# A depthwise branch's 1x1 convolution moved into the preceding scan, and two of its nine taps moved to TensorE

## The chip, the cores and the metric

The kernel runs on one core of a Trainium2 chip. Five engines work side by side, each through its own instruction queue in order: TensorE (PE in the profile; PEld is its loading of weights), VectorE (DVE), ScalarE (ACT), GpSimd (POOL) and SyncE (SP), which here issues nearly all DMAs. The metric is the device time of one execution in microseconds. Before the change it is 19043.21 us, the median of 3 runs (19038.22 to 19052.77).

## The reference

The input is x, eight images of 384 channels and 64 x 64 pixels, in float32. Two layers follow each other, both with a residual.

```python
# layer 0: channel attention on a group-normalised input
q = dwconv3x3(conv1x1(gn(x), wq), dwq)      # the same for k and v
attn = softmax(l2norm(q) @ l2norm(k).T * temperature)   # 8 heads, 48 x 48
x = x + conv1x1(attn @ v, wproj)

# layer 1: selective scan in four directions k
xs = cross_scan(gn(x))                      # rows, columns, and both reversed
dt, B, C = split(x_proj[k] @ xs)            # 12 + 16 + 16 rows
h = h * exp(dt * A) + dt * u * B            # along 4096 positions, 16 states a channel
y = sum over states of h * C, plus D * u, merged over the four directions
x = x + gelu(layernorm(y))
```

## The kernel before

For each image `channel_attention` and then `selective_scan` run. The order on each engine is written out by hand: every compute instruction is pinned to program order. x stays in SBUF as three tiles of 128 channels (NJ = 3).

**Attention.** The work is cut into 36 pieces of 16 image rows and 128 channels: 12 for k, 12 for q (each 128 channels, then four row groups), then 12 for v (each row group, then three channel groups). KQ is 24, the first v piece. The loop over t is a pipeline: in iteration t, `bands` and `band` make the 1x1 convolution of piece t+2 (three products of 512 columns on PE per eight rows, then an eviction with bias on ACT, L370 and L374) into the tile `pre`; `start_sum` and `end_sum` prepare piece t+1 (three or four whole-tile products by a tap's weight on ACT, L419, the center tap straight into the PSUM accumulator `ac`, and two additions on POOL); `finish_sum` ends piece t on DVE, with five taps as multiply-add (L457) and an addition (L462). For v, 18 rows of all three channel groups make one `pre`; two of its rows are copied from the one before. In the q and k pieces, transposes, Gram products and statistics of the previous image's output (`load_last`, tile `fs`) go along. In the v pieces the previous image's output is finished (`finishing`: loads `fy`, transposes, GELU, a POOL addition, the store), attention is projected (`project_in`, L603, and `project_out`, L610, a DVE addition), and the next image's statistics are taken from loads into qT and gm (`load_ahead`). The weights are scaled by the normalisation's 1/std (`scale_weights`), and `shift_of` makes the matching bias: nine products of one column on PE and one 128x3 instruction on DVE.

**Scan.** 32 steps (four directions of eight chunks of 512 positions), each of 12 units (three channel groups by four groups of four states). In unit u, POOL makes `db` for the next unit (L950), ACT the decays `da` (`decay`, L938), DVE four scans `h` (L962), PE the transposes of the previous unit's h (`turned`, L983), ACT copies them out (`kept`, L989, tile hc), and PE multiplies them by C (`added`, L1000; on two blocks of every fourth unit of directions 0 and 2, a `skip` product more). `weigh` makes w = x * dt (L921). Units 0 to 5 also hold the projection of the next step on PE (`project`), unit 6 its eviction (`lay_out`), and unit 9 is a burst: the next step's step sizes with two ACT table loads, the four `cp` tiles on DVE, and two of the three moves of y (`take`). One PSUM bank (`ps_m`, tag m) serves `px`, `pct` and the shift in turn. `look_ahead` prepares k's weights of the next image: the load in step 2, three scalings and the shift in step 3.

What sets the order around the change is this hand-written order and the buffers' release: nothing is scheduled later by a tool. SP's queue, too, issues in program order and waits there for what a DMA needs.

## Time and profile before

| What | Value |
|---|---|
| Median of 3 runs | 19043.21 us |
| Profiled execution, its own time | 19037.42 us |
| Its span, first to last instruction | 19035.6 us |
| Mean granted PE clock | 0.968 |
| Busy DVE, ACT, PE, POOL | 96%, 93%, 90%, 89% of the span |
| DMA | 1842.96 MB, mean 97 GB/s |
| One image: attention, then scan (image 1) | 417.1 us, 1951.7 us |

Busy time is the union of an engine's instructions. A busy share over the span is a mean over stages with different limits, so the stages are read one by one with a table of stretches: each row gives the stretch in microseconds from the span's start, its length, and busy time with the count of instructions for PE, PEld, DVE, ACT and POOL, then the granted clock of PE, the share of the 16 DMA engines in use and the rate. The view of waits gives, for an instruction, what ended the idle time before it: total, how often, the longest. The timeline gives start, length, engine, line, operation, tiles and count, and in brackets the idle time before it with what ended it. A float32 product shows as two matmul records, a transpose as one.

### The profile page before, as it was taken

The page shows a single profiled execution, that of the slowest core. Times are in us where ns is not written, and L with a number is a line of the kernel's source. Part 1 is how long each engine was busy: PE and PEld are TensorE (multiplying, and loading weights), DVE is VectorE, ACT ScalarE, POOL GpSimd, SP SyncE. Part 2 cuts the span into 40 slices and gives each one's busy share as a digit, 9 for nine tenths or more (in the row PEclk, how much of TensorE's full clock was granted, in tenths as well). Part 3 has the DMA queues.
Part 4 walks back from the last instruction along what each step waited for, and adds up shares of the span by engine and source line. Part 5 has one row for each costly group of instructions (what it writes and reads, how often), then busy time and mean ns, then how long its engine had stood idle before and what let it go on. Part 6 is the DMA issues. An engine that isn't in the chain of part 4 may idle for free. (4 is left out here: it accounts for less than half of the span.)

```text
span 19035.6 us, 415284 instructions
## 1 busy us (share of the span) xinstructions
PE 17213.2 (90%) x166560; PEld 9804.2 (52%) x166560; DVE 18353.2 (96%) x17552; ACT 17725.0 (93%) x29821; POOL 16891.1 (89%) x7491
## 2 busy tenths in 40 slices
PE   7999989999899998999989999899998999989998
PEld 4555545555455554555545555455554555545554
DVE  8999989999899998999989999899998999989999
ACT  6999979999799997999979999799997999979998
POOL 4999959999599995999959999599995999959998
PEclk9999999999999999999999999999999999999999
DMA  1233332333323333233332333223333233322333
GB/s 58 87 100 100 103 99 86 99 100 103 102 83 100 99 104 105 83 96 100 109 99 89 94 97 107 99 90 98 96 104 100 89 100 100 98 88 88 100 99 118
DMA packets 1199753, 1842.96 MB, mean 97 GB/s; under 512 B 154400, under 2 KB 1014816, under 8 KB 1060608
## 3 DMA queue, kind: packets, MB, share of 16 engines
q1 hardware_dynamic: 1196960, 1816.28, 29.8%
q8 instruction: 1314, 21.53, 0.5%
q14 instruction: 615, 5.04, 0.1%
q10 hardware_dynamic: 864, 0.12, 0.0%
HBM read 1497.29 MB, written 318.77 MB: 95 GB/s over the span
## 5 line engine op out<-in xcount | busy, mean ns | idle before, releaser
L950 POOL TENSOR_TENSOR db<-w,B 128x2048 f32<-128x2048 f32 x3072 | 14077.5, 4588 | 47.8 <-DVE h L962 24.9
L962 DVE TENSOR_TENSOR_SCAN h<-da,ca,db 128x512 f32<-128x512 f32 x10752 | 12723.9, 1265 | 30.7 <-ACT da L938 16.8
L983 PE MATMUL pt<-ident,h 128*128 128x128 f32 x49152 | 8164.9, 291 | 1079.4 <-ACT hc L989 882.1
L938 ACT ACTIVATE da<-dt,neg_a 128x512 f32<-128x512 f32 x12288 | 8616.7, 703 | 178.4 <-DVE h L962 171.3
L989 ACT COPY hc<-pt 128x512 f32<-128x512 f32 x12288 | 7265.4, 594 | 161.7 <-PE pt L983 77.0
L983 PEld LDWEIGHTS pt<-ident,h 128*128 128x128 f32 x49152 | 5324.2, 143 | 3958.9 <-ACT hc L989 2658.4
L1000 PE MATMUL py<-hc,cp 128*32 128x128 f32 x98304 | 5221.7, 289 | 1.2 <-ACT hc L989 1.2
L1000 PEld LDWEIGHTS py<-hc,cp 128*32 128x32 f32 x98304 | 1983.3, 109 | 2164.0 <-issue 2143.9
L962 DVE TENSOR_TENSOR_SCAN h<-da,db 128x512 f32<-128x512 f32 x1536 | 1739.5, 1209 | 65.1 <-ACT da L938 43.5
L426 POOL TENSOR_TENSOR pr<-pr,pr 128x1008 f32<-128x1008 f32 x288 | 673.1, 2337 | 1187.9 <-ACT pr L419 1156.8
L847 PE MATMUL px<-x,wx 128*44 128x128 f32 x6144 | 1580.2, 346 | 79.5 <-DVE cp L889 65.6
L921 POOL TENSOR_TENSOR w<-x,dt 128x512 f32<-128x512 f32 x744 | 1063.6, 1430 | 1.4 <-ACT dt L912 1.4
L847 PEld LDWEIGHTS px<-x,wx 128*44 128x44 f32 x6144 | 505.3, 120 | 663.5 <-issue 630.7
L904 PE MATMUL pd<-xd,wdt 128*128 128x512 f32 x1536 | 725.8, 608 | 97.5 <-DVE h L962 91.6
L432 POOL TENSOR_TENSOR pr<-pr,pr 128x1008 f32<-128x1008 f32 x288 | 574.9, 1996 | 230.7 <-ACT pr L419 165.2
L603 PE MATMUL pp<-v,mT 128*128 128x512 f32 x1152 | 545.7, 622 | 100.0 <-DVE v L462 98.9
L889 DVE TENSOR_TENSOR cp<-quad,pct 128x512 f32<-128x512 f32 x1024 | 630.4, 684 | 0.0
L976 POOL COPY ca<-h 128x4 f32<-128x4 f32 x2688 | 552.7, 206 | 0.0
L904 PEld LDWEIGHTS pd<-xd,wdt 128*128 128x128 f32 x1536 | 270.9, 189 | 397.4 <-issue 177.2
L912 ACT ACTIVATE dt<-pd,dt_bias 128x512 f32<-128x512 f32 x768 | 469.5, 679 | 2.1 <-PE pd L904 1.4
L1042 DVE TENSOR_TENSOR ys<-ys,py 128x512 f32<-128x512 f32 x576 | 388.5, 674 | 38.6 <-PE py L1000 38.6
L603 PEld LDWEIGHTS pp<-v,mT 128*128 128x128 f32 x1152 | 219.2, 198 | 359.3 <-issue 232.5
(337 smaller groups left out, 11426.5 us busy)
## 6 DMA issues: line engine op xcount, KB each, us to landing
B<-bcd SPq DMA_DIRECT2D x1024, 1024.0 KB, 5.1
yd<-ys SPq DMA_DIRECT2D x384, 256.0 KB, 5.3
ys<-yd SPq DMA_DIRECT2D x768, 128.0 KB, 3.0
yd<-ys SPq DMA_DIRECT2D x768, 128.0 KB, 5.2
x<-in_x SPq DMA_DIRECT2D x48, 1024.0 KB, 8.0
x1d<-x SPq DMA_DIRECT2D x192, 256.0 KB, 3.0
ys<-yd SPq DMA_DIRECT2D x192, 256.0 KB, 2.9
fy<-yd SPq DMA_DIRECT2D x128, 384.0 KB, 4.2
```

The lines of the kernel that those rows point to most:

```text
L426: pin(nc.gpsimd.tensor_add(q[:, :, 1:], q[:, :, 1:], left[:, :, : W - 1]))
L603: pin(nc.tensor.matmul(pps[m, c], lhsT=fold_of[0][:, j, bass.ts(m, P)], rhs=vs["v"][:, j, bass.ts(c, CH)], start=j == 0, stop=j == NJ - 1,))
L847: pin(nc.tensor.matmul(split(pxs[s][:XR, :])[:, part, :], lhsT=wx[:, j, k, :], rhs=view(x1[j], k, c)[:, part, :], start=i == 0, stop=i == ...
L889: pin(nc.vector.tensor_mul(t, m.broadcast_to([P, NQ, HP]), c.broadcast_to([P, NQ, HP])))
L904: pin(nc.tensor.matmul(pd, lhsT=wdt[:, k, bass.ts(j, P)], rhs=xds[s], start=True, stop=True))
L921: pin(eng.tensor_mul(split(ws[s, j]), view(x1[j], k, c), split(dts[s, j])))
L938: pin(nc.scalar.activation(t, dts[s, j], AF.Exp, scale=neg_a[:, j, steps[s][0], n : n + 1]))
L950: pin(eng.tensor_mul(t, w.broadcast_to([P, NV, CH]), bts[s, g]))
L962: pin(nc.vector.tensor_tensor_scan(h, da, db, 0.0 if start else carries[s - 1][:, j, n : n + 1], ALU.mult, ALU.add,))
L983: pin(nc.tensor.transpose(t[:, f, :], hs[u][:, bass.ts(q, HP), :].rearrange("p l v -> p (l v)"), ident))
L989: pin(nc.scalar.copy(t, pts.pop((u, lb))))
L1000: pin(nc.tensor.matmul(py[f * HP : (f + 1) * HP, lb, :], lhsT=cps[s, g][:, q, :], rhs=hc[:, f, :], start=g == lb == 0, stop=g == NG - 1 an ...
```

## The change

For all images but the first, v's 1x1 convolution is made during the scan of the image before. In steps 3 to 26 of that scan one product of 128 channels by 512 positions is made per step: an x chunk is loaded every third step in unit 2 (`v_load`), the three matmuls go at the ends of units 9, 10 and 11 (`v_product`), ACT evicts with the bias in unit 0 of the next step, and the result is stored to DRAM (`v_store`, tile v1d). Attention then loads windows of 18 rows from there (`load_v`) instead of computing bands. For these v pieces the center tap and the vertical neighbour go to PE as products with diagonal matrices (`add_by_pe`, tile `diag`, made by nine DVE instructions at the start of attention); ACT's center product and one of DVE's five taps are gone. wv is loaded, scaled and shifted in steps 0 to 3 of the scan, wk in steps 28 to 31, one scaling a step. Several buffers are fewer: hc 4 for 6, w 2 for 3, ysum 2 for 3 (its loads move to units 6, 7 and 10), the products' tag split into 2 and 2 for 4, the weights 1 for 2. In the scan's first step the third `weigh` moves from DVE to POOL.

```diff
@@ channel_attention
+            if v1_d:
+                diag = wp.tile([P, NJ, 3, P], F32, name=f"diag{b}")
+                for m in range(NJ):
+                    for k in range(3):
+                        pin(nc.vector.tensor_scalar_mul(
+                            diag[:, m, k, :], ident, dws["v"][:, m, 3 * k + 1 : 3 * k + 2]
+                        ))
+
             def load_w(n):
-                wts[n] = wp.tile([P, NJ, C], F32, tag="wt", bufs=2, name=f"{n}{b}")
+                wts[n] = wp.tile([P, NJ, C], F32, tag="wt", bufs=1 if v1_d else 2, name=f"{n}{b}")
...
+                if w == "v" and v1_d:
+                    return []
...
+            def load_v(p):
+
+                pres["v", p] = t = work.tile([P, L], F32, tag="pre", name=f"pre{b}v{p}")
+                r0, r1 = max(0, PR * p - 1), min(H, PR * (p + 1) + 1)
+                nc.sync.dma_start(
+                    t[:, : NJ * (PR + 2) * W].rearrange("p (m l) -> p m l", m=NJ)[:, :, : (r1 - r0) * W],
+                    v1_d[:, :, r0 * W : r1 * W].rearrange("m p l -> p m l"),
+                )
...
+            def add_by_pe(t):
+
+                pre, lo = rows_of(t)
+                m, y0 = pieces[t][1], PR * pieces[t][2] - lo
+                tap, dy, r0, r1 = far_tap(t)
+                for s, e in ((0, r0), (r0, BR), (BR, r1), (r1, PR)):
+                    both = r0 <= s and e <= r1
+                    for d, k in ((0, 4), (dy, tap))[: 1 + both] if e > s else ():
+                        pin(nc.tensor.matmul(
+                            accs[t][:, s:e, :], lhsT=diag[:, m, k // 3, :],
+                            rhs=pre[:, y0 + d + s : y0 + d + e, :], start=d == 0, stop=d != 0 or not both,
+                        ))
...
-                q, left = product(t, 1 if up else 7, -1 if up else 1), product(t, 3, 0)
+                q, left = product(t, 1 if up else 7, -1 if up else 1, tag="q", bufs=2), product(t, 3, 0)
...
-                product(t, 4, 0, accs[t])
+                if helped(t):
+                    add_by_pe(t)
+                else:
+                    product(t, 4, 0, accs[t])
...
-                for tap in (0, 2, 6, 8, 7 if y0 else 1):
+                for tap in (0, 2, 6, 8) + (() if helped(t) else (far_tap(t)[0],)):
...
-                elif t == 2:
+                elif t == 2 and not v1_d:
                     load_w("wv")
...
+                if v1_d and 0 <= cc < T:
+                    w, m, p = pieces[cc]
+                    if w == "q" and m > 0 and p == NP - 1:
+                        load_v(m - 1)
+                    elif w == "v" and m == NJ - 1 and p + 2 < NP:
+                        load_v(p + 2)
@@ selective_scan
-                eng = nc.vector if s == 0 else nc.gpsimd
-                ws[s, j] = work.tile([P, CH], F32, tag="w", bufs=3, name=f"w{b}_{s}_{j}")
+                eng = nc.vector if s == 0 and j < 2 else nc.gpsimd
+                ws[s, j] = work.tile([P, CH], F32, tag="w", bufs=2, name=f"w{b}_{s}_{j}")
...
-                t = work.tile([P, NF, P], F32, tag="hc", bufs=6, name=f"hc{b}_{u}_{lb}")
+                t = work.tile([P, NF, P], F32, tag="hc", bufs=4, name=f"hc{b}_{u}_{lb}")
...
+            V0 = 3
+            def next_piece(s):
+                return divmod(s - V0, NJ) if v1_d is not None and V0 <= s < V0 + NCH * NJ else None
...
+            def v_product(s, j):
+
+                if next_piece(s):
+                    c, m = next_piece(s)
+                    if j == 0:
+                        near["p"] = ps_m.tile([P, CH], F32, tag="m", name=f"pv{b}_{c}_{m}")
+                    pin(nc.tensor.matmul(
+                        near["p"], lhsT=near["v"][:, j, bass.ts(m, P)], rhs=near["x"][:, j, :],
+                        start=j == 0, stop=j == NJ - 1,
+                    ))
+
+            def v_store(s):
+
+                if next_piece(s):
+                    c, m = next_piece(s)
+                    t = work.tile([P, CH], F32, tag="va", bufs=1, name=f"va{b}_{c}_{m}")
+                    pin(nc.scalar.activation(t, near["p"], AF.Identity, bias=near["bv"][:, m : m + 1]))
+                    nc.sync.dma_start(v1_d[m, :, bass.ts(c, CH)], t)
...
-                if u == 2 * UN:
-                    near["w"] = load_wk(b + 1)
-                if u == 3 * UN + 5:
-                    scale_weights(near["w"], after[1])
-                if u == 3 * UN + 7:
-                    near["b"] = shift_of(big, ps_m, "m", near["w"], after[0], f"{b + 1}k")
+                mean, rstd = after
+                s, r = divmod(u, UN)
+                for n, w, s0 in (("v", "wv", 0), ("w", "wk", 28)):
+                    j = s - s0
+                    if j == 0 and r == 2:
+                        near[n] = load_near(b + 1, w)
+                    if 0 <= j < NJ and r == 8:
+                        pin(nc.scalar.activation(
+                            near[n][:, j, :], near[n][:, j, :], AF.Copy, scale=rstd[:, j : j + 1]
+                        ))
+                    if j == NJ and r == 7:
+                        near["b" + n] = shift_of(big, ps_m, "m", near[n], mean, f"{b + 1}{w[1]}")
...
-                if r in (2, 6, 10) and not last:
-                    sum_of(s, r // 4)
+                if r in (6, 7, 10) and not last:
+                    sum_of(s, (r - 5) // 2)
...
-                if 0 < s < S and r in (0, 2):
+                if s < S and (r == 2 or r == 0 < s):
                     weigh(s, 1 + r // 2)
...
                 kept(3, o - 1)
+                if r == 0:
+                    v_store(s - 1)
...
                     kept(2)
+                    v_product(s, 0)
                     return
...
                 added(1)
...
+                if r > 9:
+                    v_product(s, r - 9)
```

## The prediction

> **What bounds the kernel now.** I read the page's first rows, then busy time by stage, then waits by stage, then the timeline of single steps. The profiled execution took 19037.4 us (span 19035.6), 5.8 us under the median of 19043.2; sums are made against it.
>
> The busy table for image 1: channel attention, its v part alone, the denser 90 us of that part, the scan; then scan step 3 of image 1 and of image 7 (columns: stretch, its length, busy time and count of PE, PEld, DVE, ACT, POOL, granted clock, DMA share, GB/s).
>
> ```profile
> 2390.40:2807.50 417.10, 354.83 (x1280) 191.86 (x1280) 357.41 (x429) 311.77 (x441) 188.84 (x92) 0.95 0.32 105
> ...
> 2613.00:2766.00 153.00, 125.67 (x368) 60.84 (x367) 135.62 (x169) 108.58 (x165) 77.57 (x39) 0.92 0.56 186
> ...
> 2655.00:2745.00 90.00, 86.13 (x260) 41.02 (x258) 78.02 (x92) 73.82 (x114) 53.91 (x27) 1.00 0.78 257
> ...
> 2807.00:4759.00 1952.00, 1798.31 (x19540) 1034.37 (x19540) 1933.66 (x1761) 1904.53 (x3292) 1925.51 (x846) 0.97 0.30 96
> ...
> 2993.30:3058.80 65.50, 59.13 (x642) 35.80 (x641) 60.95 (x57) 61.41 (x107) 61.02 (x30) 0.95 0.23 79
> 17208.50:17269.20 60.70, 56.03 (x620) 33.18 (x620) 60.70 (x56) 59.63 (x104) 60.62 (x29) 0.97 0.26 85
> ```
>
> See: the scan is 1952 us of an image and DVE has no gap there (99%); POOL is at 99%, ACT at 98%, PE at 92%. Whatever enters the scan enters a stage where four engines are nearly full, and the room is a matter of single microseconds per step of 60.7. In attention, DVE carries k and q; in the dense v stretch PE is at 96% and DVE at 87%.
>
> Step 3 is 4.8 us longer in image 1 than in image 7, which has no next image to prepare. The waits of DVE in that step, in image 1:
>
> ```profile
> DVE bias2k L277 <- PE pb2k L272: 3.8, 1, 3.8
> DVE h L962 <- ACT da L938: 0.7, 1, 0.7
> ```
>
> See: one 128x3 instruction stands in DVE's order ahead of the scans and waits 3.8 us for PE's weight-times-mean product; all scans queue behind it.
>
> The third thing is what one late engine costs. PE, ACT and DVE in step 4 of image 1, around the burst (unit 9) and units 10 and 11:
>
> ```profile
> 3107.76 1.09 PE L983 MATMUL pt<-ident,h 128*128 128x128 f32 x8
> 3111.12 1.11 PE L983 MATMUL pt<-ident,h 128*128 128x128 f32 x4 [2.27 <-ACT hc L989]
> 3112.17 0.66 PE L1000 MATMUL py<-hc,cp 128*32 128x128 f32 x8
> ```
> ```profile
> 3115.54 0.59 ACT L989 COPY hc<-pt 128x512 f32<-128x512 f32 x1 [0.45 <-PE pt L983]
> ...
> 3117.70 0.59 ACT L989 COPY hc<-pt 128x512 f32<-128x512 f32 x1 [0.98 <-PE pt L983]
> ```
> ```profile
> 3118.91 1.28 DVE L962 TENSOR_TENSOR_SCAN h<-da,ca,db 128x512 f32<-128x512 f32 x1 [0.53 <-ACT da L938]
> ```
>
> See: PE idles 2.27 us in the burst, then four transposes take 1.11 us instead of 0.66: the clock is halved. PE falls behind, ACT loses 0.45 + 0.98 = 1.43 us to it, and DVE stops for 0.53. So ACT stands about 0.9 us ahead of DVE here: that much delay of ACT is free, and more is paid in full.
>
> **The change part by part**, per image; seven images (1 to 7) get the new attention, seven scans (0 to 6) the new work.
>
> *v stage of attention.* DVE loses one tap in 12 pieces: 12 x 1.262 (tap row) = 15.2 us. PE loses 27 band products and gains 54 diagonal ones. A full product is 0.86 us (three in 2.74, band row); a piece drops two bands, 5.2 us, and gains 31 or 32 rows of 64 = 3.4 us, so PE is 1.8 us lighter per piece. In the dense stretch (about seven pieces) PE gives 12 and DVE 8.9; I take DVE's. Outside it DVE leads and gives 6.3. ACT loses the center product (1.1) and two evictions (0.69 each) a piece and is not the bound. Against it:
> - Four loads of three 18-row windows, 1.77 MB, 5.4 us each at the 326 GB/s of the busiest 8 us. The first goes to SP's queue behind piece 19 and ahead of a 384 KB load for the last image's statistics, which lands in 3.2 us; 8.6 of the 9 us until DVE asks: 0 to 3, I take 0.7. The fourth falls into the dense stretch, 69.6 us of DMA in 90; with it 75 in some 80: 0 to 6, I take 1.5. The others find the queue at 0.2 to 0.5.
> - PE instead of ACT now waits for the accumulator bank that DVE frees, with transposes and projections queued behind it, whose results DVE adds. The 3.4 + 0.8 + 2.6 us behind that release end at 7; DVE, with bn_stats, taps and one addition first, asks at 7.8. Nothing, by 0.8 us.
> - Nine diagonal tiles on DVE, 0.28 each (row qT<-ident,roots): 2.5 us inside the 9.1 us in which DVE waits for fs, whose load SP issues 1.6 us after dwv. If fs came early they would cost 2.5.
>
> Sum: 15.2 - 2.2 = **13 less**, between 5 and 17 (17 if PE's 12 counts in full). Seven times: -91.
>
> *A second shift in the scan.* wv's is put in step 3, wk's moves to step 31. The seven present ones cost 4.1 to 4.9 (step 3 of images 0 to 6 against 60.7), 4.0 of it wait and instruction; the rest is the three scalings in a row, now one a step. New: 4.0 + 3.5 (no skip products ahead of PE in step 31) - 4.5 = +3. Removing wv's from attention gives nothing, it waited there 0.8 in image 0 alone. +21 (14 to 28).
>
> *Third weigh of step 0 moves to POOL*, 1.43 us (row L921). POOL is 49.0 of 49.0 busy from 2811 to 2860, so it delays the scans; DVE's 0.69 saved lies before a wait of 2.6 us for B. 8 x 1.4 = +11 (0 to 13).
>
> *One product a step in 24 steps.* PE 3 x 0.86, ACT one eviction (0.69 busy, 0.6 of pace), SP one store and every third step a load; their 12.6 MB add 8 GB/s to 96. SP waits for ACT at unit 0 and has y's moves, not due before unit 4, behind it. The first matmul stands in the burst and waits for the bank that the last cp leaves at 3476.6 in the step shown next; it fits PE's idle time from 3476.0 to 3478.3. The other two end units 10 and 11. ACT takes 1.10 a pair of copy and decay, PE 0.94 at full clock (transposes started at 3119.17 and 3120.11), and stands some 0.5 to 0.9 ahead: 8 pairs give 1.2, so 1.72 is covered. In the 13 steps with skip products (0.49 each, two in these units) PE comes 0.7 to 0.9 short, with the eviction 1.3 to 1.5 against the cushion of 0.9 to 1.3: 0.3 each, 4 us. Against that the product splits PE's idle 2.3 us into 0.7 and 0.7; I take it that the clock then mostly stays up. DVE's waits for ACT are 60.2 us over the run, 7.5 an image; I credit 2. Net +2, x 7 = +14 (bounds -2 and +25 an image).
>
> The halving itself, by stretch (after burst of step 10):
>
> ```profile
> 3475.90:3478.30 2.40, 0.14 (x3) 0.02 (x1) 2.40 (x4) 2.39 (x5) 2.40 (x3) 1.00 0.83 276
> 3478.30:3481.70 3.40, 3.31 (x28) 2.16 (x28) 3.40 (x4) 3.40 (x7) 3.32 (x2) 0.67 0.98 263
> ```
>
> A gap of 2.3 us is followed by 0.67. The Trainium skill ("TensorE: Matmul & The Clock Gate", What's actually happening) has the clock halve only after an idle window of about 3.4 us; this trace disagrees, a shorter gap does it. By the page the gap would cost nothing and filling it would bring nothing: my credit of 2 would go and the sum would be 14 us higher. I go by the rows.
>
> *Smaller buffers.* hc 6 to 4: PE's transposes of copy n follow its products of copy n-3, so the buffer of n-4 is free. w 3 to 2: POOL writes and reads it in order. ysum 3 to 2, loads at units 6, 7, 10: the last waits for a store issued in unit 9, due a step later. pr 4 to 2 and q 2: ACT may start sooner, DVE binds there. One weight buffer instead of two: wproj's load waits for q's last band, over by then. The new eviction loads no table, as L374 shows none. Nothing each; uncovered, at most the 0.3 a step that DVE idles now, 77 us in all.
>
> Sum: -91 + 21 + 11 + 14 = **-45**: 18992 on the profiled execution, 18998 beside the median.
>
> **Rivals.**
> - *PE's clock stays halved in units 10 and 11.* For: 0.67 above, in two steps of three. Then the product of unit 10 takes 1.7, ACT's cushion is gone every step and at least the 0.9 us of eviction and product is paid: 24 x 7 x 0.9 = 151, 19150. It turns the sign from 45 / 168 = 0.27 us a step on. Against: the longest gap left is 0.7.
> - *The v stage turns DMA-bound* and gives half: 7 x 6.5 = 45 lost, 19043. For: DMA at 0.78 with 1.77 MB more in less time. Against: DVE waits 0.2 us on DMA there now.
> - *DVE gets no relief*: PE's diagonal products come too late by what the tap saved, as the margin is 0.8. Attention gives 0: 19089. Against: PE is lighter.
> - *Everything is covered*, PE's relief counts (17) and the products cost -2: -119 + 32 - 14 = -101, 18942.
>
> **How the numbers follow.** Mine 0.46, clock 0.17, DMA 0.15, no relief 0.10, all covered 0.12. A measurement tells 0.2%, 38 us, from no change: under 19005 is faster. Mine spans 18965 to 19030, two thirds below 19005 (0.31); with the last 0.43. The DMA case and a third of mine are within; clock and no relief above: same 0.28, slower 0.29. The range drops half of the clock case and a little below: 18940 to 19130; without the other sign 18940 to 19043.
>
> **What would show it.** v pieces about 1.1 us shorter each; two DVE waits of 3 to 4 us for pb in images 0 to 6; step 0 longer by 1.4; steps 3 to 26 at 60.7 to 61.2, a granted clock near 1.0 after the burst. I am wrong if DVE waits for ACT in every step's units 11 to 3, or if DVE in the v pieces waits for PE's accumulator or for a DMA.

## The result

The changed kernel takes 19115.99 us (median of six executions, 19104.37 to 19127.69), the kernel before, run beside it, 19043.44 (six, 19038.22 to 19052.77): a ratio of 1.0040, 95% interval 1.0029 to 1.0052. It is slower by some 73 us; the forecast was 45 faster. The profiled execution took 19127.69 us with a span of 19125.7, 90 over that of before (mean granted clock 0.972 for 0.968); it is the slowest of the six, so some 12 of the 90 are its own. By the starts and ends of the scans in the two profiles these 90 us are

| Part | Before | After | Difference | Forecast |
|---|---|---|---|---|
| Up to the first scan | 444.3 | 445.9 | +1.6 | 0 |
| Attention of images 1 to 7, sum | 2936.9 | 2960.5 | +23.6 | -91 |
| Scans of images 0 to 7, sum | 15584.7 | 15649.8 | +65.1 | +46 |

So, by these two profiles, 115 of the missing 135 us were lost in attention, 19 in the scan. Of attention's 23.6 the v part has 8.7 (3.0 in each of images 1 to 6, 9.3 gained in image 7). Another 13 come from k's pieces, mostly one of them: they take 84.6 to 88.2 us from image to image, and 84.6 to 87.8 in the kernel before. Their mean over images 1 to 6 is 85.3 before and 87.6 in the changed kernel, but 85.3 again in E5 and E13, whose attention is the changed kernel's. So those 13 are scatter. Against the forecast some 100 us were lost in the v part.

The busy table for the changed kernel, image 1: attention, its v part, pieces 5 to 8 of the v part, the scan, step 3 (columns as before: stretch, its length, busy time and count of PE, PEld, DVE, ACT, POOL, granted clock, DMA share, GB/s).

```profile
2400.50:2825.00 424.50, 348.73 (x1208) 191.00 (x1208) 343.21 (x424) 282.91 (x397) 188.45 (x92) 0.90 0.36 120
2630.00:2779.00 149.00, 116.69 (x335) 57.47 (x334) 115.46 (x150) 83.86 (x129) 76.15 (x41) 0.88 0.67 225
...
2692.50:2748.30 55.80, 42.24 (x122) 20.64 (x122) 42.90 (x52) 33.33 (x52) 31.11 (x16) 0.85 0.85 286
...
2825.00:4783.00 1958.00, 1836.47 (x19702) 1044.46 (x19702) 1934.79 (x1761) 1905.30 (x3318) 1926.90 (x847) 0.99 0.32 102
...
3015.70:3079.30 63.60, 58.62 (x634) 34.87 (x637) 60.84 (x57) 59.80 (x103) 60.85 (x29) 1.00 0.23 82
```

The same table of the kernel before for the same four pieces, 5 to 8:

```profile
2681.00:2731.00 50.00, 46.16 (x139) 21.46 (x138) 47.87 (x54) 43.34 (x67) 30.96 (x16) 1.00 0.87 286
```

See: every engine has less to do in these pieces (PE 42.2 for 46.2, DVE 42.9 for 47.9, ACT 33.3 for 43.3), and they take longer, 55.8 us for 50.0. The last two columns are alike, 0.85 and 286 GB/s against 0.87 and 286. At 286 GB/s the two stretches carry 15.96 and 14.30 MB; the difference, 1.66 MB, is the fourth window load (1632 KB by the list of DMA issues, 1.67 MB), and 1.66 MB / 286 GB/s is the 5.8 us that the stretch grew. That the sum comes out so exactly is in part luck, since the rate varies from image to image. But the other images say the same: images 4 and 5 of the changed kernel, the longest and the shortest of the six,

```profile
9836.48:9895.35 58.87, 42.21 (x122) 20.81 (x122) 42.95 (x51) 33.41 (x52) 31.11 (x16) 0.83 0.81 275
12226.22:12280.73 54.51, 40.95 (x122) 19.91 (x122) 42.76 (x51) 33.45 (x52) 30.94 (x16) 0.87 0.87 297
```

carry 16.2 MB each, the one at 275, the other at 297 GB/s, with the same work on VectorE. In the kernel before it is the other way round: the four pieces take 50.0 to 50.3 us in all six images while the rate goes from 270 to 288. There VectorE, 47.9 us busy, sets the time, with the DMAs not far behind.

The waits of DVE in the v part of image 1 (what waited, for what; total, times, longest):

```profile
DVE x L657 <- PE pp L650: 15.0, 7, 7.2
DVE st L710 <- DMA qT<-in_x: 10.9, 1, 10.9
DVE v L509 <- PE pa L540: 4.2, 1, 4.2
DVE helper L294 <- ACT roots L289: 0.5, 1, 0.5
```

Before, in the same part: pp 11.7 (longest 3.9), qT 0.2, pa 1.5. The timeline around the longest wait, SP's issues and then DVE:

```profile
2705.60 0.44 SPq L414 DMA_DIRECT2D pre1v<-v1d  x1
...
2713.34 1.18 SPq L254 DMA_DIRECT2D out<-fy  x1
2718.75 0.36 SPq L214 DMA_DIRECT2D fy<-x1d  x1
2719.17 1.47 SPq L659 DMA_DIRECT2D x1d<-x  x3
2720.68 0.79 SPq L702 DMA_DIRECT2D qT<-in_x  x1
```
```profile
2715.57 0.70 DVE L658 BATCH_NORM_STATS2 st<-x 128x6 f32<-128x512 f32 x1
2727.16 1.28 DVE L710 BATCH_NORM_STATS2 st<-qT 128x6 f32<-128x512 f32 x2 [10.89 <-DMA qT<-in_x]
```

See: the window load goes out at 2705.6, the load of x for the next image's statistics (qT) only at 2720.7, and DVE stands until 2727.2 with taps, projections and statistics behind it in its order. In between SP, which issues in order, waits for the finished image's stores to land (2700 to 2722):

```profile
SPq L214 <- DMA out<-fy: 9.5, 3, 4.4
```

The scan's two steps with a shift, waits of DVE in step 3 and step 31 of image 1:

```profile
DVE bias2v L277 <- PE pb2v L272: 2.8, 1, 2.8
```
```profile
DVE bias2k L277 <- PE pb2k L272: 2.1, 1, 2.1
```

And PE after the burst of step 10 of image 1:

```profile
3490.76 1.09 PE L1036 MATMUL pt<-ident,h 128*128 128x128 f32 x8
3492.51 1.13 PE L1146 MATMUL pv<-xa,wv 128*128 128x512 f32 x2 [0.66 <-DVE cp L942]
3494.32 0.66 PE L1036 MATMUL pt<-ident,h 128*128 128x128 f32 x4 [0.69 <-ACT hc L1042]
```

See: the product cuts PE's idle stretch into 0.66 and 0.69 us, and the four transposes behind it take 0.66, where they took 1.11 after a gap of 2.27.

Time per piece, from the ends of DVE's final additions, is the finest measure of the v part. Means of images 1 to 6 in us, and the part's sum in image 7, which has no next image and so no load_ahead; the kernels of the experiments are in the same table. Profiles of the same attention code differ by up to 1.8 us in the sum of images 1 to 6 (E5 and E13 157.2, E14 155.9 beside the changed kernel's 157.7; E12 155.3 and E4 155.0 beside the 154.7 of before), and by 3 in image 7 (144.0 to 147.2):

| Kernel | v pieces 0 to 11 | Sum | Image 7 |
|---|---|---|---|
| before | 10.3 10.5 14.4 9.2 26.4 11.3 13.1 14.3 11.3 13.8 11.2 8.9 | 154.7 | 153.3 |
| after | 14.3 9.2 12.9 7.7 26.1 10.0 12.1 23.7 10.0 11.7 12.4 7.6 | 157.7 | 144.0 |
| E1 thirds | 14.6 9.2 12.9 7.7 26.1 10.0 12.2 23.2 10.9 11.7 12.4 7.6 | 158.5 | 144.1 |
| E2 taps back | 9.4 10.5 14.2 9.0 21.1 11.3 13.0 23.1 11.3 12.6 14.7 8.9 | 159.0 | 145.4 |
| E3 scan only | 10.3 10.5 14.2 9.0 26.4 11.3 13.1 14.3 11.3 15.3 13.6 8.9 | 158.1 | 154.6 |
| E6 half loaded | 13.7 9.2 12.9 7.7 26.1 10.0 12.0 16.4 11.7 12.3 12.4 7.6 | 152.1 | 148.2 |
| E7 diagonals late | 11.1 9.2 14.6 7.7 23.7 10.0 11.6 23.5 10.0 11.4 12.8 8.0 | 153.7 | 137.3 |
| E9 ahead later | 14.5 9.2 12.9 7.7 26.1 10.0 12.2 12.5 10.0 13.7 12.3 9.9 | 150.9 | 147.2 |
| E10 all and ahead later | 11.2 9.2 14.2 7.7 23.7 10.7 11.6 13.0 10.0 13.0 13.8 9.9 | 147.8 | 138.6 |

See in the first two rows: pieces 1, 3, 5, 8 and 11 are shorter by the tap (1.3 to 1.5). Piece 7 is 9.4 longer, piece 0 is 4.0 longer, piece 4 has gained nothing, piece 10 is 1.2 longer. If every piece had gained the tap's 1.3, piece 7 would be 10.7 shorter than it is, pieces 0 and 4 together 6.3 and piece 10 2.5.

### The profile page after: what moved, and what is told of

Its sections match the earlier page's. It is cut to its first block, busy times and chain, and to the rows that moved or that the text cites. A ratio compares the mean times of both kernels' runs of the same rounds, so it can differ in the third digit from the quotient of the medians.

```text
span 19125.7 us, 417079 instructions
## 1 busy us (share of the span) xinstructions
PE 17456.7 (91%) x167190; PEld 9883.6 (52%) x167190; DVE 18270.4 (96%) x17523; ACT 17531.4 (92%) x29695; POOL 16906.5 (88%) x7499
## 5 line engine op out<-in xcount | busy, mean ns | idle before, releaser
L1003 POOL TENSOR_TENSOR db<-w,B 128x2048 f32<-128x2048 f32 x3072 | 14053.9, 4579 | 58.7 <-DVE h L1015 37.4
L991 ACT ACTIVATE da<-dt,neg_a 128x512 f32<-128x512 f32 x12288 | 8672.8, 707 | 144.0 <-DVE h L1015 135.6
L1036 PE MATMUL pt<-ident,h 128*128 128x128 f32 x49152 | 8037.7, 287 | 760.2 <-ACT hc L1042 543.4
L1036 PEld LDWEIGHTS pt<-ident,h 128*128 128x128 f32 x49152 | 5269.0, 142 | 3793.3 <-ACT hc L1042 2385.5
L1053 PE MATMUL py<-hc,cp 128*32 128x128 f32 x98304 | 5166.9, 286 | 1.2 <-ACT hc L1042 1.2
L1146 PE MATMUL pv<-xa,wv 128*128 128x512 f32 x1008 | 562.9, 640 | 91.8 <-DVE cp L942 91.7
L925 POOL COPY cy<-cx 64x128 f32<-64x128 f32 x256 | 116.3, 454 | 473.6 <-DMA cx<-bcd 454.7
```

The lines of the kernel that those rows point to most:

```text
L991: pin(nc.scalar.activation(t, dts[s, j], AF.Exp, scale=neg_a[:, j, steps[s][0], n : n + 1]))
L1003: pin(eng.tensor_mul(t, w.broadcast_to([P, NV, CH]), bts[s, g]))
L1036: pin(nc.tensor.transpose(t[:, f, :], hs[u][:, bass.ts(q, HP), :].rearrange("p l v -> p (l v)"), ident))
L1053: pin(nc.tensor.matmul(py[f * HP : (f + 1) * HP, lb, :], lhsT=cps[s, g][:, q, :], rhs=hc[:, f, :], start=g == lb == 0, stop=g == NG - 1 an ...
```

## The experiments

Ratios are to the kernel before, run beside each. The changed kernel stands at 1.0040.

### E1: the window load in thirds

```diff
-                    elif w == "v" and m == NJ - 1 and p + 2 < NP:
-                        load_v(p + 2)
+                    elif w == "v":
+                        i, part = divmod(NJ * p + m - (NJ - 1), NJ)
+                        if 0 <= i < NP - 2:
+                            load_v(i + 2, (part, part + 1))
```

> The changed kernel with one edit: the third and the fourth load of v's windows (1.63 MB each) are cut into one load per 128 channels, and the three are issued after three successive pieces instead of together. Theory (the large load stands on the rings ahead of a store of the finished image, SP waits for that store, and the load of the next image's statistics behind it comes late): v piece 7, 22.7 to 26.4 us in images 1 to 6, returns to about 13, the wait of DVE for qT of 10.9 us in image 1 falls under 2; 6 x 10 us = 60 less, some 19055. Rival (the late qT is the volume of DMA in the dense stretch, or the wait is replaced by one for TensorE): piece 7 stays over 20 or the same microseconds return as waits for pp; 19095 to 19120.

Measured: 19121.09 us, ratio 1.0045 (1.0032 to 1.0057), the rival. Piece 7 stays at 23.2; DVE's waits around it in image 1:

```profile
DVE st L714 <- DMA qT<-in_x: 13.9, 3, 11.2
DVE x L661 <- PE pp L654: 11.4, 5, 7.1
```

The wait of qT is 11.2 where it was 10.9. My first theory, a single large load ahead of small ones, fell: the size of one load is not the cause. The bytes stayed the same.

### E2: v's taps as before

```diff
             def helped(t):
-                return bool(v1_d) and pieces[t][0] == "v"
+                return False
```

The diagonal tiles go too.

> The changed kernel with v's taps as before the change: the centre product on ScalarE, five taps on VectorE, no diagonal tiles; v still comes from DRAM. Theory (the taps' gain is real and paid: 12 taps of 1.26 us, 15.2 us an image, but part of it goes to waits of DVE for pp and pa behind the diagonal products, 11.7 to 25.4 us for pp in image 1): the v part gets 15 us longer by the taps and gets back the 14 us of pp waits, so within 5 us an image either way; 19080 to 19150. Rival (the diagonal products cost nothing but what the trace names as DMA): 7 x 15 = 105 longer, 19220. Rival (TensorE is what the attention waits for): shorter, under 19060.

Measured: 19121.57 us, 1.0043 (1.0029 to 1.0057), as the first theory had it: an image has twelve taps more on DVE, 15 us, and its v part takes 159.0 for 157.7. The pieces say why. Without diagonal products piece 0 falls from 14.3 to 9.4 and piece 4 from 26.1 to 21.1, nearly 10 us that these products cost where DVE waits for PE. And piece 7 is 23.1 all the same, so they are not its cause; nor is VectorE's work, as the tap more in each piece left it as long. DVE's waits for PE in image 1:

```profile
DVE x L650 <- PE pp L643: 4.9, 5, 1.7
DVE v L502 <- PE pa L533: 1.4, 1, 1.4
```

### E3: the scan's part alone

```diff
-                x_next = x_next, (*after, near["w"], near["bw"], v1_d)
+                x_next = x_next, (*after, near["w"], near["bw"], None)
```

> The scan's part of the change alone: v's convolution of the next image runs in the scan and is stored, with both shifts and the smaller buffers, but nobody reads it; attention computes v with its own bands and five taps as before (its ScalarE products keep the smaller rings of the changed kernel). Theory (by the scans' lengths, 15649.8 against 15584.7 us in the two profiles): 65 us over the kernel before, 19108; what is left to the changed kernel, some 8 to 25 us, is attention's. Rival (what the scan gained in length came from a late start, and follows the attention): under 19080.

Measured: 19134.63 us, 1.0051 (1.0038 to 1.0064), 96 over before where 65 were expected. The scans of images 0 to 6 take 1955.7 us on average (before 1948.8, after 1957.2), as they should; but the attention did not stay as before: pieces 9 and 10 are 15.3 and 13.6 for 13.8 and 11.2 (E4 and E12, with the attention of before, have 14.5 and 11.2). In pieces 9 to 11 of image 1 DVE waits 3.0 us for qT, 0.2 before:

```profile
DVE st L710 <- DMA qT<-in_x: 3.0, 1, 3.0
DVE x L657 <- PE pp L650: 2.3, 1, 2.3
```

In attention only the smaller rings of ACT's products (the buffers that they use in turn) are left of the change in this kernel. So, by exclusion, their cover was not complete: about 3 us an image in the v part. That was not tried by itself, and how a smaller ring makes qT late was not traced. By the medians the changed kernel is 0.1% faster than this one, but the two intervals overlap, so a gain from attention's part of the change is not shown.

### E4: the side edits of the scan alone, in the kernel before

```diff
-                ws[s, j] = work.tile([P, CH], F32, tag="w", bufs=3, name=f"w{b}_{s}_{j}")
+                ws[s, j] = work.tile([P, CH], F32, tag="w", bufs=2, name=f"w{b}_{s}_{j}")
-                t = work.tile([P, NF, P], F32, tag="hc", bufs=6, name=f"hc{b}_{u}_{lb}")
+                t = work.tile([P, NF, P], F32, tag="hc", bufs=4, name=f"hc{b}_{u}_{lb}")
-                if r in (2, 6, 10) and not last:
-                    sum_of(s, r // 4)
+                if r in (6, 7, 10) and not last:
+                    sum_of(s, (r - 5) // 2)
-                eng = nc.vector if s == 0 else nc.gpsimd
+                eng = nc.vector if s == 0 and j < 2 else nc.gpsimd
```

> The kernel before with only the side edits of the change in the scan: hc 6 to 4, w 3 to 2, ysum 3 to 2 with y's loads at units 6, 7 and 10, and the third weighing of step 0 on GpSimd. No convolution of v in the scan. Theory from the last image, which has no next image and yet grew from 1943.4 to 1949.5 us: 8 x 6.1 = 49 longer, 19092. Rival (the prediction: only the weighing costs, 8 x 1.4 = 11): 19054.

Measured: 19058.16 us, 1.0010 (1.0001 to 1.0019), some 19 longer: nearer the prediction's 11 than the 49 of the trace theory. Images 1 to 6 have scans of 1948.6 us for 1949.2; step 0 alone is longer, 65.4 for 64.1, which gives 10 us in eight scans. The profiled execution, 19045.64, lies 13 under the median, so where the rest of the 19 stands is not shown. The premise of the 49, that the last image's scan grew by 6 us, was no effect of an edit: that same code takes 1942.4 us in E7's profile, 1944.4 in E3's and 1950.4 in E1's.

### E5: the bias instruction behind the scans

```diff
+        def take_it():
+            pin(nc.vector.tensor_scalar_mul(bias, pb[:, :NJ], -1.0))
...
                 look_ahead(u)
                 unit(u)
+                while later:
+                    later.pop()()
```

> The changed kernel with both shifts' VectorE instruction (128x3, the bias) put behind the four scans of unit 7 instead of ahead of them; the nine small products on TensorE stay where they are. Theory (DVE's wait for pb is paid in full by the scans behind it): step 3 falls from 63.6 to about 61, step 31 from 60.6 to about 58.5, 7 x 4.7 = 33 less than the changed kernel: 19083. Rival (the wait only moves, since the products themselves hold up TensorE's transposes, or the bank of pb is held longer and the next C waits for it): both steps within 0.5 us of now, 19116.

Measured: 19082.62 us, 1.0023 (1.0014 to 1.0033), as expected. Step 3 falls from 63.6 to 61.9, step 31 from 60.6 to 58.7, 26 of the 33 us in seven images. No wait for pb is left in step 3; one of 1.4 us for ACT's decays stands there instead, which is why it does not reach 60.7:

```profile
DVE h L1022 <- ACT da L998: 1.4, 2, 1.2
```

### E6: half of the window loads left out

```diff
-                        load_v(p + 2)
+                        pres["v", p + 2] = pres["v", 1]
```

> The changed kernel without the third and the fourth load of v's windows (1.63 MB each): the lower half of v is computed from the second window, so only the first half of v is right. Theory (the dense stretch of the v part is bound by its DMA volume, cutting the load into thirds therefore changed nothing): without the volume piece 7 falls from 23.7 to 12.5 to 14 us and pieces 8 to 11 stay; 6 x 10 = 60 less than the changed kernel, 19056. Rival (piece 7 waits for something that the new order of TensorE's or SP's work brings, not for the volume): piece 7 stays over 20 us, 19110.

Measured: 19093.78 us, 1.0029 (1.0018 to 1.0040), a third of what was expected. Piece 7 falls by 7.3 us to 16.4, pieces 8 and 9 give 2.3 of it back, the sum falls from 157.7 to 152.1. These 5.6 us are what the one load of 1.67 MB in this stretch costs at 286 to 300 GB/s (5.6 to 5.8): the edit leaves all but the loads as it was, and this is the most direct sign that the bytes are paid. The other 4 us an image that the expectation wanted were not the load's. DVE still waits there, now for gm:

```profile
DVE st L710 <- DMA gm<-in_x: 5.5, 2, 4.0
```

Pieces 5 to 8 of image 1:

```profile
2691.74:2741.54 49.80, 40.69 (x122) 19.87 (x122) 42.85 (x51) 33.45 (x52) 31.53 (x16) 0.93 0.88 300
```

Even without the load the stretch runs at 0.88 and 300 GB/s, and VectorE, busy 42.9 of 49.8 us, does not fill it.

### E7: the diagonal products later in PE's order

```diff
-                if helped(t):
-                    add_by_pe(t)
-                else:
+                if not helped(t):
                     product(t, 4, 0, accs[t])
...
                 if t == KQ + 3:
                     project()
+                if 0 <= cb < T and helped(cb):
+                    add_by_pe(cb)
```

> The changed kernel with the diagonal products issued later in TensorE's order: behind the grams, the transposes of the finished image and the projection of the same iteration, instead of ahead of them. Theory (TensorE, waiting in order for the accumulator bank, holds up the grams and projections that VectorE needs: piece 0 at 11.7 to 16.3 us against 10.3 before, piece 4 at 26 against 20.7 where the diagonal products are absent, waits for pp 25.4 us in image 1 against 11.7): piece 0 falls by 2 to 4, piece 4 by 2 to 5, some 5 us an image, 19080. Rival (the stretch is bound by DMA, and whatever is gained ahead of piece 7 is waited there): under 10 us of change in all, 19106 to 19126.

Measured: 19074.20 us, 1.0017 (1.0007 to 1.0026), 42 less than the changed kernel by the medians: the theory. Piece 0 falls from 14.3 to 11.1, piece 4 from 26.1 to 23.7; piece 2 grows by 1.7. PE's waits for the accumulator bank in image 1, changed kernel:

```profile
PE ac L452 <- DVE v L509: 9.5, 3, 7.4
...
PE ac L452 <- issue: 4.7, 1, 4.7
```

are gone here, and DVE's longest wait for pp falls from 7.2 to 3.2:

```profile
DVE st L708 <- DMA qT<-in_x: 10.9, 1, 10.9
DVE x L655 <- PE pp L648: 10.1, 7, 3.2
DVE ac L502 <- PE ac L452: 3.3, 4, 1.4
DVE v L507 <- PE pa L538: 2.7, 1, 2.7
```

The first line is untouched: PE's order and the late qT are two separate losses. In image 7, which has no load_ahead, the v part is now 137.3 us against 153.3 before, 16 less.

### E8: four edits together

The edits of E5 and E7, the third weighing of step 0 on VectorE at unit 4, and windows by 128 channels as soon as their place is free:

```diff
-                    elif w == "v" and m == NJ - 1 and p + 2 < NP:
-                        load_v(p + 2)
+                    elif w == "v" and p + 2 < NP:
+                        pres["v", p + 2] = pres["v", p]
+                        load_v(p + 2, (m, m + 1))
```

> The changed kernel with four edits: both shifts late as in e5, the diagonal products late as in e7, v's windows loaded by 128 channels as soon as the same place of the window two before is free (6 loads of 0.54 MB, the first of them 48 us earlier than now), and the third weighing of step 0 on VectorE again, at unit 4. Theory: 33 for the shifts, 35 for the diagonal products, 8 x 1.1 = 9 for the weighing and 3 to 5 an image, 25, for the earlier loads: 102 less than the changed kernel, 19014, under the kernel before by 25. Rival (the volume of DMA in the dense stretch takes back what the v part gains): only the shifts and the weighing count, 19074.

Measured: 19036.65 us, 1.0000 (0.9991 to 1.0009). 79 of the 102 expected came: piece 7 is still 20.1 on average (17.9 to 22.1), so the earlier loads moved few bytes out of the stretch: pieces 5 to 8 of image 1 still carry 16.2 MB (54.5 us at 297 GB/s).

### E9: the loads for the next image's statistics out of the dense stretch

```diff
-                if t > KQ + 2:
+                if t > KQ + 2 and t not in (KQ + 5, KQ + 6):
                     load_ahead()
```

> The changed kernel, in which two of the six rounds of load_ahead (two 512 KB pieces of the next image's x each, for its statistics) are taken out of the dense stretch: none after pieces 5 and 6 of v, instead two more after pieces 9 and 10, where the DMA share falls under 0.55. Theory (the dense stretch, DMA 0.86 over 60 us in image 1, ends late by its volume): piece 7 falls from 23.7 to about 13, as in the last image, which has no load_ahead (12.5); pieces 9 to 11 grow by at most 2.5 each, since VectorE is free to wait there less; 6 x 8 = 48 less than the changed kernel, 19068. Rival (whatever leaves piece 7 comes back in pieces 8 to 11 or in the tail): 19106 to 19126.

Measured: 19071.78 us, 1.0018 (1.0009 to 1.0027), as expected. Piece 7 is 12.5, the value of the last image; pieces 9 and 11 take back 2.0 and 2.3, since the statistics now stand there. Pieces 5 to 8 of image 1:

```profile
2704.60:2748.80 44.20, 38.32 (x122) 18.80 (x122) 38.25 (x42) 33.34 (x52) 31.11 (x16) 1.00 0.87 292
```

The rate is 292 GB/s at 0.87, near that of the changed kernel, but the bytes are 12.9 MB for 15.9, and the time went with them, 44.2 us for 55.8. The image has the same instructions and the same bytes in all. Some of the work moved along: VectorE is busy 38.3 us here for 42.9, which pieces 9 and 11 take back. What is left, 6.8 us in the sum of the v part, comes from the loads' new place. The four pieces now take 44.2 to 45.0 us in all six images while the rate goes from 287 to 311 GB/s, so the DMAs no longer set their time.

### E10 and E11: towards a faster kernel

E10 joins E8 and E9. E11 adds ScalarE's eviction one place later:

```diff
                 kept(3, o - 1)
-                if r == 0:
-                    v_store(s - 1)
...
                 decay(i0 + 3)
+                if r == 0:
+                    v_store(s - 1)
                 kept(0)
```

> The four edits of e8 and that of e9 together. Theory: e8's piece 7 (17.9 to 22.1 us) falls to about 13, 6 x 6 = 36 less than e8: 19000, ratio 0.998 to the kernel before. Rival (the gain returns in the later pieces): as e8, 19037.

> As e10, with ScalarE's eviction of v's product in unit 0 moved behind the second of the unit's decays instead of ahead of them. Theory (ScalarE waits there 0.2 to 0.66 us a step for the product, and at the changes of direction, steps 7 to 9, 16, 17 and 23 to 25, that reaches the scans): up to 3 us an image, 7 x 3 = 21 less than e10: 18979. Rival (at these steps it is TensorE's or GpSimd's work that is late, or the next projection now waits for the bank): within 10 us of e10.

Measured: 19031.88 us, 0.9996 (0.9988 to 1.0005), and 19028.23 us, 0.9994 (0.9985 to 1.0002). Neither can be told from the kernel before. Both expectations, 19000 and 18979, were missed, and the rivals' numbers came. E10's piece 7 did fall, to 13.0, and attention is 26 us less than E8's in the profiles; but E10's scans are 9 us longer there, and the medians are 5 us apart. E10's attention comes to 414.6 us in images 1 to 6 (before 420.3) and to 400.1 in image 7 (415.1). E11's eviction gave step 17 back (61.2 to 60.8) and left steps 23 to 25 as they were.

### E12: the late bias in the kernel before

The edit of E5, made in the kernel before, nothing else.

> The kernel before with its one shift late as in e5, nothing else. Theory (the 3.8 us that VectorE waits for pb in step 3 are paid by the scans): step 3 falls from 65.3 by 2.5 to 3.8 us, 7 x 3 = 21 less: 19016, and so close to what e10 can bring. Rival (step 3 is held by the three scalings on ScalarE as well): under 7 us less, 19031.

Measured: 19031.03 us, 0.9998 (0.9989 to 1.0007): step 3 falls by 1.2 us only, from 65.3 to 64.1. The rival's number. That the three scalings hold step 3 up instead was not tried by itself. With this edit alone the kernel before is within 3 us of E11: the change with everything mended, E11, brings nothing that can be measured.

### E13 and E14: which engine pays for the products

E13 stores x's chunk without an eviction; E14 evicts x's chunk without a product.

```diff
-                    pin(nc.scalar.activation(t, near["p"], AF.Identity, bias=near["bv"][:, m : m + 1]))
-                    nc.sync.dma_start(v1_d[m, :, bass.ts(c, CH)], t)
+                    nc.sync.dma_start(v1_d[m, :, bass.ts(c, CH)], near["x"][:, m, :])
```
```diff
-                    pin(nc.tensor.matmul(
-                        near["p"], lhsT=near["v"][:, j, bass.ts(m, P)], rhs=near["x"][:, j, :],
-                        start=j == 0, stop=j == NJ - 1,
-                    ))
...
-                    pin(nc.scalar.activation(t, near["p"], AF.Identity, bias=near["bv"][:, m : m + 1]))
+                    pin(nc.scalar.activation(t, near["x"][:, m, :], AF.Identity, bias=near["bv"][:, m : m + 1]))
```

> The changed kernel without ScalarE's evictions of v's product: what is stored for v is the loaded chunk of x itself, so the output is not the reference's; the products, loads and stores stay, with the same bytes. Theory (ScalarE, 98% busy in the scan, pays the eviction and its wait where TensorE's projections with strided reads have already used up its lead): steps 7, 8, 16, 17, 23, 24 and 25 return to the values without products (61.1, 60.1, 58.2, 60.7, 61.0, 60.0, 60.9), 5 us an image, 7 x 5 = 35 less than the changed kernel: 19081. Rival (TensorE's 2.6 us): these steps stay, within 1.5 us an image, 19106 to 19116. Rival (the DMAs): all stay, 19116.

> The changed kernel without TensorE's products for v: the eviction on ScalarE reads the loaded chunk of x with the same form and stores it, so the output is not the reference's. Theory (ScalarE's eviction): of the 5 us an image at most the wait for the product goes, 1 to 2 us, 19102 to 19109. Rival (TensorE): steps 7 to 9, 16, 17 and 23 to 25 return to the values without products, and the clock's halving after the burst comes back in most steps; 19081 or, by the halving, up to 19095. Rival (the DMAs): as the changed kernel.

Measured: E13 19109.19 us, 1.0041 (1.0026 to 1.0056); E14 19096.16 us, 1.0034 (1.0022 to 1.0045). By the medians the two can't be told apart from the changed kernel; the steps can (means of images 1 to 6; E4 is the scan without products):

| Step | 7 | 8 | 16 | 17 | 23 | 24 | 25 | Scan |
|---|---|---|---|---|---|---|---|---|
| E4 | 61.05 | 60.14 | 58.23 | 60.74 | 61.03 | 59.95 | 60.86 | 1948.6 |
| after | 61.89 | 60.86 | 58.96 | 61.63 | 62.07 | 60.92 | 61.49 | 1957.6 |
| E13, no eviction | 61.94 | 60.83 | 58.97 | 60.94 | 62.12 | 61.04 | 61.59 | 1955.9 |
| E14, no product | 61.32 | 60.33 | 58.63 | 60.70 | 61.26 | 60.59 | 61.28 | 1952.5 |

The scans of the six other profiles with the whole work in them (E1 to E3, E6, E7 and E9) come to 1955.8 to 1956.8, and step 17 to 61.2 to 61.5 there. So E13's scan is no shorter than theirs, and E14's is by 3 to 4. My theory, ScalarE's eviction, fell but for 0.3 to 0.5 us of step 17; it is TensorE's product. The bytes are the same in both, so the DMAs are not it. Step 23 of image 1, in E13 and in E14:

```profile
4229.40:4291.50 62.10, 59.75 (x630) 33.53 (x626) 60.92 (x56) 59.26 (x104) 59.15 (x19) 1.00 0.30 96
```
```profile
4227.60:4288.70 61.10, 57.73 (x616) 32.75 (x615) 60.68 (x56) 59.30 (x104) 59.19 (x19) 0.97 0.30 102
```

PE is busy 59.8 of 62.1 us with the product and 57.7 of 61.1 without. Of the 9.0 us between E4 and the changed kernel 5.1 are the product's by these profiles, or 3 to 4 against the six others. The second shift has 0.9 of the rest (steps 3 and 31 against the same steps of E4); 3 to 4 us remain unassigned.

## Why the prediction was wrong, point by point

- **The v stage, -13 an image.** Wrong, and the step that failed is "The fourth falls into the dense stretch ... 0 to 6, I take 1.5", together with "In the dense stretch (about seven pieces) PE gives 12 and DVE 8.9; I take DVE's". The v part grew by 3.0 us in images 1 to 6. I read the DMA column over 90 us, 0.78 and 257 GB/s, priced the load by the best 8 us, 326 GB/s, and took DVE's wait of 0.2 us as room. Over pieces 5 to 8 alone the kernel before already ran at 0.87 and 286 GB/s, with VectorE setting the time and the DMAs close behind. With the load in it the DMAs set the time: the load costs its bytes over the rate, 5.8 us (5.6 by E6), and the taps saved on DVE in these four pieces, 4 x 1.26 = 5.0, bring nothing. Pieces 5, 6 and 8 do get shorter, and piece 7 gives it back: 5.8 + 5.0 = 10.8 are its missing 10.7. Both terms of the sum fall together. The rival named the mechanism, "The v stage turns DMA-bound", but gave it half the gain and 0.15.
- The Trainium skill ("DMA: Bandwidth & Descriptors", Bandwidth) lists 341 GB/s for a load of 1 MB and 425 for one of 16 MB, issued from GpSimd. By these figures the window load would cost 3.9 to 4.9 us, as an estimate. This stretch of mixed loads and stores, issued from SP, held 275 to 298 GB/s in the changed kernel, and the measured rate decides.
- The same page (Rules for kernel authors) asks for at least 1 MiB a DMA for the most bandwidth; cutting the load into thirds of 544 KB in E1 changed nothing that could be measured, in either direction.
- **"Nothing, by 0.8 us" for PE behind the accumulator bank.** Wrong: 4.0 us an image in the v part of images 1 to 6 (157.7 to 153.7 in E7), 6.7 in image 7. The margin was worked out for one dense piece; the loss is at piece 0, where the last Gram products stand behind, and at piece 4, where the finished image's transposes start. E2, without the diagonal products, gets 9.9 us back at these two.
- **The tap itself, 12 x 1.262.** Right (15.1 us, where the sum has 15.2): pieces without another wait are 1.3 to 1.5 shorter, and with the diagonal products late and no load_ahead the part is 16 shorter (E7, image 7).
- **Smaller buffers, nothing each.** Right for the scan (E4: scans of 1948.6 for 1949.2, though step 0 in them is 1.3 longer), wrong in attention by about 3 us an image, by exclusion ACT's product rings (E3); piece 10's missing 2.5 are the 2.4 that it grew there.
- **The nine diagonal tiles, nothing.** Right: they take 1.85 us, ahead of a wait of 4.1 for `fs`, and the time from the scan's end to the first finished piece is 28.5 us for 28.6.
- **The third weighing on POOL, 1.4 a scan.** Right: 1.2 (step 0 from 64.1 to 65.3), and 0.6 to 0.7 of it returns in E8 and E10.
- **The second shift, +3 an image.** Too high: step 31 is 2.3 longer as foreseen in kind, but step 3 is 1.7 shorter without two of the scalings, +0.7. DVE's waits of 2.8 and 2.1 for pb stand where they were put, at a smaller size. The reading behind it, that 4.0 of the present 4.1 to 4.9 us are this wait and its instruction, did not hold: with the instruction out of the way (E12) step 3 got 1.2 shorter.
- **The products, +2 an image.** The term was mis-sized: with the rest of the scan's growth taken off, 6 to 8, and 3 to 5 of it TensorE's by E14. I spread 0.3 over 13 steps with skip products and looked for ScalarE's cushion; the time is lost in the steps next to a change of direction, where PE had more to do already: 58.2 us in step 23 before, 56.0 in a step 3 without preparation, and 59.7 of 62.0 us now. In between, steps 4 to 6 and 18 to 22 stand at 60.7 to 60.8, as forecast.
- **The clock after the burst.** Right in the mechanism: gaps of 0.66 and 0.69 us are followed by full speed, and the clock over image 1's scan is 0.99 for 0.97. Over the whole run 3.6% of the groups of four transposes took over 0.9 us before, 1.5% after, and 3.6% again in E14, where the gap is open. The rival of a halved clock in units 10 and 11 did not come. The credit of 2 us for it was not seen in the steps' length.
- That the range held the time was luck: its upper end was there for the rival of the halved clock, which did not come. The sign was wrong because the DMA rival was priced as a loss of half the gain, not of the gain and the load, and the two smaller terms (PE behind the accumulator, the products) missed in the same direction.

## What to carry to other kernels

Ask of a stretch whether its bytes over its own rate already fill it, at the length of a few pieces and not of the whole stage: at a DMA share of 0.87 VectorE did not wait yet, and still the bytes added there were paid and its saving was lost. Then move bytes: putting two rounds of loads out of the stretch (E9, 44 us) was worth as much as the best single edit of an engine's order (E7, 42). Work that is handed to another engine brings its wait with it, so put it in that engine's order behind what others need from it (E7), and a tiny instruction behind the long ones that don't need it (E5, 33 us; in the kernel before, E12, too little to tell from nothing). And ask what the mended change brings over the old kernel mended where that applies (E11 against E12): here, nothing that could be measured.

## What the runs showed beyond that

The kernels taken side by side tell which engine sets the dense stretch (pieces 5 to 8 of v; images 1 to 6, mean length and VectorE's busy time, lowest and highest of the rest):

| Kernel | Length | DVE busy | DMA share | GB/s | MB |
|---|---|---|---|---|---|
| before | 50.0 | 47.9 | 0.83 to 0.87 | 270 to 288 | 13.5 to 14.4 |
| E3 scan only | 50.0 | 47.9 | 0.83 to 0.88 | 263 to 286 | 13.1 to 14.3 |
| after | 55.8 | 42.8 | 0.81 to 0.88 | 275 to 298 | 15.9 to 16.3 |
| E2 taps back | 58.7 | 48.0 | 0.84 to 0.89 | 283 to 300 | 17.0 to 17.3 |
| E6 half loaded | 50.2 | 42.9 | 0.88 to 0.90 | 297 to 301 | 14.5 to 15.3 |
| E9 ahead later | 44.6 | 38.3 | 0.85 to 0.92 | 287 to 311 | 12.7 to 14.0 |

Where VectorE fills it (before, E3), the length stays and the rate varies. In the changed kernel the bytes stay within 3%, and the length goes against the rate. In no kernel's images did these four pieces pass 0.92 or 311 GB/s, though one stretch of 8 us of the kernel before reached 326 at 0.96. So a share of 0.87 over 50 us was already close to all that this mix of loads and stores got.

And one and the same scan, that of the last image, took 1942.4 to 1950.4 us in the eleven kernels that share its code (the changed one, E1 to E7, E9, E13 and E14); what decides it was not found, and differences of that size in one image's scan say nothing about an edit.
